# The last head's probabilities by transfers, the network's first half first, and TensorE's order written out to the end

## The chip, the core and the metric

The kernel runs on one core of a Trainium2 chip. A core has five engines that run side by side, each through its own queue of instructions in order: TensorE (matmuls and their weight loads; PE and PEld in the profile), VectorE (DVE), ScalarE (ACT), GpSimd (POOL) and SyncE (SP), which here issues the transfers (DMA). Engines wait for each other through semaphores. TensorE writes to PSUM, which VectorE and ScalarE read; everything else lies in SBUF. The metric is the device time of one execution in microseconds; before the change it is 1357.93 us, the median of 3 runs (1357.65 to 1358.64).

## The reference

One pre-norm transformer layer over 1024 tokens of 512 features, in float32, with 32 heads of 128:

```python
x = x + attention(layernorm(x), wq, wkv, wo)
x = x + ffn(layernorm(x), k0, s0, k1, s1, k2, s2)

# attention: q, k, v = products with wq, wkv
scores = einsum('bqhd,bkhd->bhqk', q[..., :DN], k) * scale
scores = where(causal, scores, NEG_INF)
attn = einsum('bhqk,bkhd->bqhd', softmax(scores), v).reshape(B, S, H * DV)
return einsum('bse,ed->bsd', attn, wo)

# ffn: conn_dense(k, x) = x @ where(k, 1, -1); ei_dense also weighs the last fifth of the inputs
h = relu(s0 * conn_dense(k0, x)) * 2
h = relu(ei_dense(h, k1, s1, P)) * 2
return ei_dense(h, k2, s2, P)
```

The second layer norm needs a token's whole row, that is, the output of all heads for that token; the network then works on each token alone.

## The kernel before

*Tiles.* The 1024 tokens are 8 tiles of 128 (`NT`), in two halves of 4 (`TPB`, half `qb` 0 and 1). Heads go in pairs (`G` = 2, 16 pairs). The main loop (line 689) has one step for each head and query tile: `steps` lists `(h, qt)`.

*One softmax step* (`probabilities`, line 503). TensorE writes the scores of query tile `qt` against the keys it may see, `(qt + 1) * 128` columns, to the PSUM tile `sc`. There is one such tile (pool `ps_sc`, one buffer), so the next step's scores wait until this one has been read. VectorE adds the mask and takes the row minimum of the negated scores (line 518, `nmax`); ScalarE takes the exponential and its row sum (529), VectorE the reciprocal (533), ScalarE scales (534).

*Turning the probabilities.* The product with v needs the keys on the partitions, so each tile has to be transposed. For heads 0 to 30 `transpose_blocks` (540) transposes blocks of 32 x 32 on VectorE into the tile `tb0` or `tb1` (for a half), and `exchange` (575), once a half is complete, moves the blocks to their places in `pT0` or `pT1` with 16 transfers on SP's queue. `attend` (588) follows 4 steps (half 0) or 6 steps (half 1) after that: its matmuls `ps_av` and a VectorE copy (619) give `attn`. For head 31 `transpose_last` (548) does whole transposes of 128 x 128 on TensorE (568) into PSUM, copied out by VectorE (573) and ScalarE (571); its query tiles run in the order 4 to 7, then 0 to 3 (line 632), and `attend` takes another branch (596 to 608).

*What fills TensorE between.* In each step the loop adds parts of two other chains: the products that make q, k and v of the next pair (`products`, seven a matrix, with sums on VectorE and ScalarE), and the output product of an earlier pair. For the last two pairs the latter is `o_unit(g, t)` (490): two matmuls for token tile `t`, added into `acc` (501), which also holds the residual. How many parts are due by a step is planned by `out_by`, `chain_end` and a count of columns (`done`, `goal`, `total`).

*The network* (from line 772). `transposed_input(k)` takes the layer norm of the four tiles of half `k`, transposes them on TensorE (`ptx_f`), and splits them in a high and a low part (`hi` on ScalarE, `lo` on VectorE); `hidden_layer` and `output_layer` multiply both parts with the sign weights, which GpSimd makes from `k0`, `k1`, `k2` in `sign_weights`. The order is: half 1 in, hidden layer 0 of half 1, half 0 in, hidden layer 1 of half 1, hidden layer 0 of half 0, output of half 1, hidden layer 1 of half 0, output of half 0.

*What sets the order.* Transfers stand in SP's queue in program order (`load`, 64). `keep_order` (68) pins an instruction to its place in the program while `pinned[0]` is true; matmuls and transposes on TensorE go through it. `pinned[0]` is set to false for the last 8 steps and what follows (line 692), where a scheduler in the build places instructions on all engines. VectorE, ScalarE and GpSimd are placed by that scheduler except in the first stage. Once built, each engine's order is fixed.

Of the kernel before, what the change touches and what calls it, by code (L numbers as in the profile page):

```python
# [8 lines left out]
F32 = mybir.dt.float32  # L9
F32R = mybir.dt.float32r  # L10
# [19 lines left out]
def kernel(  # L30
# [30 lines left out]

    pinned = [False]

    def load(dst, src):

        tc.keep_in_program_order(nc.sync.dma_start(dst, src))

    def keep_order(ins):
# [131 lines left out]
    def mean_var(mv, xt, name):  # L200

        if len(xt.shape) == 2:
            stats = small.tile([P, 6], F32, tag="stats", name=f"stats_{name}")
            keep_order(nc.vector.bn_stats(stats, xt))
        else:
            stats = small.tile([P, 2, 6], F32, tag="stats2", name=f"stats_{name}")
            for half in range(2):
                nc.vector.bn_stats(stats[:, half, :], xt[:, half, :])
        keep_order(nc.vector.bn_aggr(mv, stats))

# [11 lines left out]

    def normalise(xt, mean_rstd, name):
        xn = work.tile([P, D], F32, tag="p", name=f"xn_{name}")
        dst = xn if len(xt.shape) == 2 else xn.rearrange("p (h d) -> p h d", h=2)
        nc.vector.tensor_scalar(dst, xt, *mean_rstd, ALU.subtract, ALU.mult)
        return xn

# [13 lines left out]
    def input_statistics(t):  # L242
        mean_var(mv_a[:, t, :], x_in[:, t, :], f"a{t}")
        keep_order(
            nc.scalar.activation(std_a[:, t, :], mv_a[:, t, 1:2], AF.Sqrt, bias=eps)
        )

    def input_rows(t):
        keep_order(nc.vector.reciprocal(rstd_a[:, t, :], std_a[:, t, :]))
        keep_order(  # L250
            nc.vector.tensor_scalar(
                x_in[:, t, :],
                x_in[:, t, :],
                mv_a[:, t, 0:1],
                rstd_a[:, t, :],
                ALU.subtract,
                ALU.mult,
            )
        )

    def input_columns(t):
        pt = transposed(t, x_in[:, t, :], "a")
        keep_order(nc.scalar.copy(xnT[:, :, t * P : (t + 1) * P], pt))

# [46 lines left out]
    def qk_plain(between):  # L311
# [6 lines left out]
        for n_units in range(NT * 2 * G):  # L318
# [17 lines left out]
            if i == TPB - 1:  # L336
                keep_order(
                    nc.scalar.activation(
                        (qT, kT)[which][h][:, k * QB : (k + 1) * QB],
                        banks[n],  # L340
                        AF.Copy,
                        scale=(-scale, 1.0)[which],
                    )
                )
# [198 lines left out]

    last_pT = {}

    def transpose_last(qt, p):
        qb, i = divmod(qt, TPB)
        if i == 0:  # L550
            spare = (heads, "qT"), (heads, "qT"), (heads, "kT"), (heads, "v")
            bufs = {"kT": 3, "v": 3}
            if qb == 0:
                t = keep.tile([P, 2, 2, TPB, P], F32, tag="tb0", name="pT_last0")
                last_pT[qb] = [t[:, m] for m in range(2)]
            else:
                last_pT[qb] = [
                    pl.tile(
                        [P, 2, TPB, P], F32, tag=tag, name=f"pT_last{m}", bufs=bufs.get(tag)
                    )  # L560
                    for m, (pl, tag) in enumerate(spare)
                ]
        for m in range(qt // 2 + 1):
            chunks = range(2 * m, min(2 * m + 2, qt + 1))
            n = len(chunks)
            ps = ps_st.tile([P, 2, P], F32, tag="st", name=f"ps_pT{qt}_{m}")
            for kc in chunks:
                nc.tensor.transpose(ps[:, kc % 2, :], p[:, kc * P : (kc + 1) * P], ident)
            dst = last_pT[qb][m][:, :n, i, :]
            if m % 2:  # L570
                nc.scalar.copy(dst, ps[:, :n, :])
            else:
                nc.vector.tensor_copy(dst, ps[:, :n, :])

    def exchange(h, qb):
# [12 lines left out]
    def attend(h, qb, pT):  # L588
# [6 lines left out]
        dst = attn[h, qb]  # L595
        if h == H - 1:
            ps = ps_mm.tile([P, TPB, P], F32, tag="mm", name=f"ps_av{h}_{qb}")
            for kc in range(nk):
                first = max(0, kc - qb * TPB)
                matmul(  # L600
                    ps[:, first:, :],
                    lhsT=vs[h][:, kc, :],
                    rhs=last_pT[qb][kc // 2][:, kc % 2, first:, :],
                    start=(kc == 0),
                    stop=(kc == nk - 1),
                )
            nc.vector.tensor_copy(dst.rearrange("p (t i) -> p t i", t=TPB), ps)
            return
        ps = ps_mm.tile([P, NB, TPB, B32], F32, tag="mm", name=f"ps_av{h}_{qb}")
# [18 lines left out]

    steps = [(h, qt) for h in range(H) for qt in range(NT)]
    steps[-NT:] = [(H - 1, (qt + TPB) % NT) for qt in range(NT)]
    to_attend = {}
    w_sign = {}

    def softmax_step(h, qt):
        p = probabilities(h, qt)
        if h < H - 1:
            transpose_blocks(h, qt, p)
        else:  # L640
            transpose_last(qt, p)

# [7 lines left out]
    PRODUCT, O_PART = 2.0, 1.0  # L650
    ATTEND_AFTER = (TPB, TPB + 2)

    pinned[0] = True
    def first_blocks():
        for t in tb:
            keep_order(nc.vector.memset(t, 0.0))
        softmax_step(*steps[0])
# [13 lines left out]
        }  # L671
    )
    load_o_weights(0)

# [14 lines left out]
    for i, (h, qt) in enumerate(steps):  # L689
        g, j = divmod(h, G)  # L690
        s = i % (G * NT)
        pinned[0] = i + 1 < len(steps) - NT
        if s == 0:
            n_chain = 21 if g + 1 < NG else 7
            o_cols = O_PART if g + 1 < NG else 2 * O_PART
            n_out = 0 if g == 0 else 14 if g + 1 < NG else NT

            if g + 2 < NG:
                out_by = [max(0, (14 * (t - 2) + 12) // 13) for t in range(G * NT)]
            elif g + 2 == NG:  # L700
                out_by = [0, 0, 0, 2, 4, 6, 6, 8, 10, 12, 13, 14, 14, 14, 14, 14]
            else:
                out_by = [max(0, t - NT + 1) for t in range(G * NT)]
            done, chain_done, out_done = 0.0, 0, 0
            total = (
                2 * G * sum(score_cols(t) for t in range(NT))
                + PRODUCT * n_chain
                + o_cols * n_out
            )
            chain_end = 14 if g + 1 < NG else 6  # L710
        if s == 0:
# [61 lines left out]
        if h == H - 1:  # L773
            if qt == 0:
                attend(h, 1, None)
            if qt == 1:
                for t in range(TPB, NT):
                    o_unit(g, t)
        if h == H - 1 and s == NT:
# [23 lines left out]
    x_parts, h1, h2 = {}, {}, {}  # L803
    for k, tag in ((1, "pT1"), (0, "tb1")):
        x_k = keep.tile([P, 2, NC, QB], F32R, tag=tag, name=f"x{k}")
        x_parts[k] = h2[k] = (x_k[:, 0], x_k[:, 1])
    h1[1] = (part(keep, "pT0", "h1_hi1"), part(pairs, "wraw", "h1_lo1", 2))

    def transposed_input(k):
        tiles = range(k * TPB, (k + 1) * TPB)  # L810
        stats = statistics([xs[t] for t in tiles], f"f{k}")
        hi, lo = x_parts[k]
        for t, st in zip(tiles, stats):
            pt = transposed(t, normalise(xs[t], st, f"f{t}"), "f")
            cols = slice((t % TPB) * P, (t % TPB + 1) * P)
            nc.scalar.copy(hi[:, :, cols], pt)
            nc.vector.tensor_tensor(
                lo[:, :, cols], pt, hi[:, :, cols].bitcast(F32), ALU.subtract
            )

    n_ps = [0]
# [7 lines left out]
    def hidden_layer(i, k, src, dst):  # L829
        hi, lo = dst  # L830
        for oc in range(NC):
# [13 lines left out]
            nc.vector.tensor_copy(h_hi, h)  # L845
            nc.vector.tensor_tensor(h_lo, h, h_hi.bitcast(F32), ALU.subtract)

    def output_layer(k):
# [30 lines left out]
    h1[0] = (part(keep, "tb0", "h1_hi0"), part(heads, "qT", "h1_lo0", 2))  # L879
# [42 lines left out]
```

## Time and profile before

| | us |
|---|---|
| median of 3 runs | 1357.93 |
| the profiled execution, its time | 1358.12 |
| its span, first to last instruction | 1356.34 |
| TensorE busy | 1342.3 |
| VectorE busy | 807.6 |
| ScalarE busy | 496.5 |
| GpSimd busy | 262.5 |

The page gives each engine's busy time, and then groups of instructions: line, engine, operation, what is written and read, how many, busy time and the mean of one, and the engine's idle time before them with what ended it. A matmul in float32 is two passes in the trace. The chain of waits is followed back from the last instruction to what released each step. In a timeline a row has the start and the length in us from the span's start. Most of TensorE's groups have line 74, the helper that records every matmul, so they are told apart by the tile they write: `sc` scores, `ps_av` the product with v, `ps_o` output units, `ps_pT` the transposes of head 31, `ptx_f` those of the network's input, `ps_h` and `ps_out` its layers.

### The profile page before, as it was taken

To read this page: it belongs to the slowest core of one execution; us is meant where nothing else is said; L and a number is where in the kernel's file an instruction comes from. 1 tells how busy PE (TensorE), PEld (TensorE's weight loads), DVE (VectorE), ACT (ScalarE), POOL (GpSimd) and SP (SyncE) were. 2 spreads that over 40 slices of the span, in tenths; PEclk is the share of its full clock that TensorE was granted. 3 is DMA by queue.
4 is the path that set the end of the run, shared out by engine and by line. 5 is a ranking of instruction groups with operands and counts; after the bars stand their busy time and mean duration, and the time that the engine had idled before them with its cause. 6 is when DMAs were issued, how large, how long until landed. Compare 5 with 4: busy or idle time off the path is not lost.

```text
span 1356.3 us, 16289 instructions
## 1 busy us (share of the span) xinstructions
PE 1342.3 (99%) x5564; PEld 869.7 (64%) x5564; DVE 807.6 (60%) x1661; ACT 496.5 (37%) x922; POOL 262.5 (19%) x324
## 2 busy tenths in 40 slices
PE   8999999999999999999999999999999999999998
PEld 7747575665757566575756657575665756657567
DVE  5455565656656565565656566565656556686475
ACT  3434333333433333343433333333333333335321
POOL 3411122211212221021222102122120212110200
PEclk9999999999999999999999999999999999999999
DMA  5356454445646444564644556454455645446301
GB/s 187 78 109 125 89 127 96 95 97 103 140 84 129 97 88 101 109 141 80 129 93 88 108 109 127 87 127 94 88 116 109 127 83 118 87 83 128 67 0 63
DMA packets 259506, 139.26 MB, mean 103 GB/s; under 512 B 18272, under 2 KB 253280, under 8 KB 259424
## 3 DMA queue, kind: packets, MB, share of 16 engines
q1 hardware_dynamic: 259424, 138.22, 48.6%
q8 instruction: 45, 0.74, 0.2%
q14 instruction: 37, 0.30, 0.1%
HBM read 38.54 MB, written 2.10 MB: 30 GB/s over the span
## 4 chain that ended last, share of the span: by engine, by line
PE 99%; DVE 0%; DMA 0%; ACT 0%; issue 0%; ACTq 0%
PE sc L74 18%; PE ps_av L74 18%; PE ps_o L74 15%; PE Y_v L74 6%; PE Y_k L74 6%; PE Y_q L74 6%; PE Z_v L74 4%; PE X_v L74 4%; PE X_q L74 4%; PE Z_q L74 4%; PE Z_k L74 4%; PE X_k L74 4%; PE ps_qk L74 2%; PE ps_h L74 2%; PE ps_out L74 1%; PE ptx_a L232 0%
## 5 line engine op out<-in xcount | busy, mean ns | idle before, releaser
L529 ACT ACTIVATE p<-p,nmax 128x128 f32<-128x128 f32 (+7 forms) x256 | 198.4, 775 | 675.3 <-DVE nmax L518 673.2
L74 PE MATMUL sc<-kT,qT 128*128 128x512 f32 (+3 forms) x768 | 290.1, 487 | 1.4 <-DVE nmax L518 1.4
L74 PE MATMUL ps_av<-pT,v 128*128 128x512 f32 x744 | 250.3, 486 | 0.0
L518 DVE CUSTOM_DVE_ANT_0 p<-sc,mask 128x128 f32<-128x128 f32 (+7 forms) x256 | 191.3, 747 | 90.4 <-PE sc L74 90.4
L540 DVE STREAM_TRANSPOSE tb<-p 128x128 f32<-128x128 f32 (+1 forms) x248 | 187.3, 769 | 75.5 <-ACT p L534 72.0
L534 ACT ACTIVATE p<-p,rtotal 128x128 f32<-128x128 f32 (+7 forms) x256 | 196.5, 773 | 78.5 <-DVE rtotal L533 78.4
L74 PEld LDWEIGHTS ps_av<-pT,v 128*128 128x128 f32 x744 | 141.1, 190 | 127.7 <-issue 103.0
L74 PEld LDWEIGHTS sc<-kT,qT 128*128 128x128 f32 x768 | 138.7, 190 | 90.0 <-issue 77.5
L481 DVE TENSOR_TENSOR acc<-acc,ps_o 128x512 f32<-128x512 f32 x190 | 128.7, 683 | 56.1 <-PE ps_o L74 50.9
L74 PE MATMUL ps_o<-wo,attn 128*128 128x256 f32 (+1 forms) x400 | 110.7, 414 | 0.3 <-DVE attn L619 0.3
L533 DVE RECIPROCAL rtotal<-total 128x1 f32<-128x1 f32 x256 | 40.5, 158 | 112.8 <-ACT p L529 112.4
L74 PEld LDWEIGHTS ps_o<-wo,attn 128*128 128x128 f32 x400 | 73.3, 190 | 31.0 <-issue 24.2
L442 POOL TENSOR_TENSOR at<-attn,attn 128x512 f32<-128x512 f32 x14 | 17.7, 1267 | 348.4 <-DVE attn L619 348.4
L619 DVE COPY attn<-ps_av 128x512 f32<-128x512 f32 x62 | 42.2, 681 | 49.8 <-PE ps_av L74 49.8
L74 PEld LDWEIGHTS X_v<-wv,xnT 128*128 128x128 f32 x512 | 62.2, 192 | 5.1
L74 PE MATMUL X_v<-wv,xnT 128*128 128x128 f32 x512 | 62.3, 275 | 0.0
L74 PEld LDWEIGHTS ps_o<-osum,at 128*128 128x128 f32 x224 | 42.5, 190 | 22.8 <-issue 19.1
L74 PE MATMUL X_q<-xnT,wq 128*128 128x512 f32 x120 | 56.4, 593 | 0.0
L74 PE MATMUL X_k<-xnT,wk 128*128 128x512 f32 x120 | 56.4, 592 | 0.0
L291 POOL TENSOR_TENSOR wsumk<-wk 128x256 f32<-128x256 f32 x15 | 10.9, 727 | 234.3 <-PE Z_v L74 156.0
L74 PE MATMUL ps_o<-osum,at 128*128 128x256 f32 x224 | 55.0, 379 | 0.0
L529 ACT ACTIVATION_READ_ACCUMULATOR p<-p,nmax 128x1 f32 x256 | 47.7, 186 | 0.0
(146 smaller groups left out, 1637.3 us busy)
## 6 DMA issues: line engine op xcount, KB each, us to landing
pT<-tb SPq DMA_DIRECT2D x496, 128.0 KB, 3.1
pT<-tb SPq DMA_DIRECT2D x496, 64.0 KB, 2.1
wq<-in_L_attn_wq_dram SPq DMA_DIRECT2D x32, 256.0 KB, 3.3
wk<-in_L_attn_wkv_dram SPq DMA_DIRECT2D x32, 256.0 KB, 3.9
wv<-in_L_attn_wkv_dram SPq DMA_DIRECT2D x16, 512.0 KB, 4.0
wo<-in_L_attn_wo_dram SPq DMA_DIRECT2D x16, 512.0 KB, 3.7
x_in<-_attn_hidden_states_dram SPq DMA_DIRECT2D x8, 256.0 KB, 5.3
acc<-_attn_hidden_states_dram SPq DMA_DIRECT2D x8, 256.0 KB, 6.6
```

What stands on the lines that cost most here:

```text
L74: keep_order(nc.tensor.matmul(*args, **kw))
L291: nc.gpsimd.tensor_tensor(t[:, 0], a(1, 0), a(1, 1), ALU.add)
L442: nc.gpsimd.tensor_tensor(t0, b(0, 1), b(0, 0), ALU.subtract)
L481: nc.vector.tensor_tensor(dst, dst, ps, ALU.add)
L518: nc.vector.tensor_tensor_reduce(out=p[:, :n], in0=sc[:, :n], in1=mask[:, S - n :], scale=1.0, scalar=BIG, op0=ALU.add, op1=ALU.min, accum ...
L529: nc.scalar.activation(p[:, :n], p[:, :n], AF.Exp, bias=nmax, scale=-1.0, accum_out=total)
L533: nc.vector.reciprocal(rtotal, total)
L534: nc.scalar.activation(p[:, :n], p[:, :n], AF.Copy, scale=rtotal)
L540: nc.vector.transpose(tb[qb][:, : qt + 1, :, i, :], p[:, :n].rearrange("p (c b k) -> p c b k", b=NB, k=B32))
L619: nc.vector.tensor_copy(dst.rearrange("p (t a i) -> p a t i", a=NB, i=B32), ps)
```

## The change

Head 31 is treated as the other heads: `transpose_last` and its branch of `attend` go, its query tiles run from 0 to 7, and its probabilities go through `tb0`, `tb1` and two exchanges. Of the last pair `attend` for half 0 comes 6 steps after the half is complete, in place of 4. The plan of the last pair is another (`out_by`, `chain_end` 9 in place of 6): five of the eight output units of the pair before are handed out during the steps, three are left for the end. After the loop half 0 comes first: `attend` of head 31's half 0, the four output units of half 0 with the layer norm of each tile by itself (`network_input`, statistics of one tile in place of four), whose transposes and splitting (`columns`) stand among the output units; then hidden layer 0 of half 0, `attend` of half 1 and its four units, hidden layer 1 of half 0 with the four transposes of half 1 after its third group, hidden layer 0 of half 1, output of half 0, hidden layer 1 of half 1, output of half 1. `pinned[0]` stays true to the end, so all of TensorE's order is that of the program; the pins on VectorE and ScalarE in the first stage go through `keep_first`, which stops after that stage. Several of the network's tiles lie in other buffers.

```diff
+    def keep_first(ins):
+        if first_stage[0]:
+            tc.keep_in_program_order(ins)
...
-    def transpose_last(qt, p):
...
-            for kc in chunks:
-                nc.tensor.transpose(ps[:, kc % 2, :], p[:, kc * P : (kc + 1) * P], ident)
...
-    steps[-NT:] = [(H - 1, (qt + TPB) % NT) for qt in range(NT)]
...
     def softmax_step(h, qt):
-        p = probabilities(h, qt)
-        if h < H - 1:
-            transpose_blocks(h, qt, p)
-        else:
-            transpose_last(qt, p)
+        transpose_blocks(h, qt, probabilities(h, qt))
...
-    ATTEND_AFTER = (TPB, TPB + 2)
+    def attend_after(h, qb):
+        return TPB if qb == 0 and h < H - 2 else TPB + 2
...
-        pinned[0] = i + 1 < len(steps) - NT
...
-                out_by = [max(0, t - NT + 1) for t in range(G * NT)]
+                out_by = [0, 0, 1, 1, 2, 2, 3, 3, 4, 4, 4, 5, 5, 5, 5, 5]
...
-            chain_end = 14 if g + 1 < NG else 6
+            chain_end = 14 if g + 1 < NG else 9
...
-        if qt % TPB == TPB - 1 and h < H - 1:
+        if qt % TPB == TPB - 1:
             qb = qt // TPB
-            to_attend[i + ATTEND_AFTER[qb]] = (h, qb, exchange(h, qb))
+            to_attend[i + attend_after(h, qb)] = (h, qb, exchange(h, qb))
...
+    def network_input(t):
+        k, i = divmod(t, TPB)
+        pl, tag, bufs = (work, "p", 3) if k == 0 else (heads, "kT", 3) if i < 3 else (heads, "qT", 4)
+        xn = pl.tile([P, D], F32, tag=tag, name=f"xn_f{t}", bufs=bufs)
+        normalise(xn, xs[t], statistics([xs[t]], f"f{t}_")[0])
+        hi, lo = x_parts[k]
+        cols = slice(i * P, (i + 1) * P)
+        def columns():
+            pt = transposed(t, xn, "f")
+            nc.scalar.copy(hi[:, :, cols], pt)
+            nc.vector.tensor_tensor(
+                lo[:, :, cols], pt, hi[:, :, cols].bitcast(F32), ALU.subtract
+            )
+        return columns
...
-    attend(H - 1, 0, None)
-    transposed_input(1)
-    for t in range(TPB):
-        o_unit(NG - 1, t)
-    hidden_layer(0, 1, x_parts[1], h1[1])
-    transposed_input(0)
-    hidden_layer(1, 1, h1[1], h2[1])
...
-    hidden_layer(0, 0, x_parts[0], h1[0])
-    output_layer(1)
-    hidden_layer(1, 0, h1[0], h2[0])
-    output_layer(0)
+    first, second = (to_attend[i] for i in sorted(to_attend))
+    attend(*first)
+    columns = {}
+    for t in range(TPB):
+        o_unit(NG - 1, t)
+        columns[t] = network_input(t)
+        if t >= 2:
+            columns[t - 2]()
+    next(o_chain)
+    columns[2]()
+    next(o_chain)
+    columns[3]()
+    next(o_chain)
+    for _ in hidden_layer(0, 0, x_parts[0], h1[0]):
+        pass
+    attend(*second)
+    for t in range(TPB, NT):
+        o_unit(NG - 1, t)
+        columns[t] = network_input(t)
+    for oc, _ in enumerate(hidden_layer(1, 0, h1[0], h2[0])):
+        if oc + 2 == NC:
+            for t in range(TPB, NT):
+                columns[t]()
+    for _ in hidden_layer(0, 1, x_parts[1], h1[1]):
+        pass
+    output_layer(0)
+    for _ in hidden_layer(1, 1, h1[1], h2[1]):
+        pass
+    output_layer(1)
```

More of the change, by code (lines that the diff above doesn't have):

```diff
@@ L60 @@
     wo_v = wo.rearrange("(h p) d -> p h d", p=P)
-    pinned = [False]
+    pinned, first_stage = [False], [True]
     def load(dst, src):
         tc.keep_in_program_order(nc.sync.dma_start(dst, src))
+    def keep_first(ins):
+        if first_stage[0]:
+            tc.keep_in_program_order(ins)
     def keep_order(ins):
@@ L203, in mean_var @@
             stats = small.tile([P, 6], F32, tag="stats", name=f"stats_{name}")
-            keep_order(nc.vector.bn_stats(stats, xt))
+            keep_first(nc.vector.bn_stats(stats, xt))
         else:
@@ L208, in mean_var @@
                 nc.vector.bn_stats(stats[:, half, :], xt[:, half, :])
-        keep_order(nc.vector.bn_aggr(mv, stats))
+        keep_first(nc.vector.bn_aggr(mv, stats))
     def statistics(tiles, name):
@@ L221, in statistics, with normalise @@
         return [(mv[:, t, 0:1], rstd[:, t, :]) for t in range(n)]
[L223 to L227, printed above, removed]
+    def normalise(xn, xt, mean_rstd):
+        nc.vector.tensor_scalar(
+            xn.rearrange("p (h d) -> p h d", h=2), xt, *mean_rstd, ALU.subtract, ALU.mult
+        )
     def transposed(t, xn, name):
@@ L243, in input_statistics @@
         mean_var(mv_a[:, t, :], x_in[:, t, :], f"a{t}")
-        keep_order(
+        keep_first(
             nc.scalar.activation(std_a[:, t, :], mv_a[:, t, 1:2], AF.Sqrt, bias=eps)
@@ L248, in input_rows @@
     def input_rows(t):
-        keep_order(nc.vector.reciprocal(rstd_a[:, t, :], std_a[:, t, :]))
-        keep_order(
+        keep_first(nc.vector.reciprocal(rstd_a[:, t, :], std_a[:, t, :]))
+        keep_first(
             nc.vector.tensor_scalar(
@@ L262, in input_columns @@
         pt = transposed(t, x_in[:, t, :], "a")
-        keep_order(nc.scalar.copy(xnT[:, :, t * P : (t + 1) * P], pt))
+        keep_first(nc.scalar.copy(xnT[:, :, t * P : (t + 1) * P], pt))
     def B(j, k):
@@ L336, in qk_plain @@
             if i == TPB - 1:
-                keep_order(
+                keep_first(
                     nc.scalar.activation(
@@ L542, in transpose_blocks @@
         )
-    last_pT = {}
-    def transpose_last(qt, p):
[L549 to L555, printed above, removed]
-            else:
[L557 to L566, printed above, removed]
-            for kc in chunks:
[L568 to L573, printed above, removed]
     def exchange(h, qb):
@@ L595, in attend @@
         dst = attn[h, qb]
[L596 to L608, printed above, removed]
         ps = ps_mm.tile([P, NB, TPB, B32], F32, tag="mm", name=f"ps_av{h}_{qb}")
@@ L636, in softmax_step @@
     def softmax_step(h, qt):
-        p = probabilities(h, qt)
-        if h < H - 1:
-            transpose_blocks(h, qt, p)
-        else:
-            transpose_last(qt, p)
+        transpose_blocks(h, qt, probabilities(h, qt))
     def score_cols(qt):
@@ L655, in first_blocks @@
         for t in tb:
-            keep_order(nc.vector.memset(t, 0.0))
+            keep_first(nc.vector.memset(t, 0.0))
         softmax_step(*steps[0])
@@ L672 @@
     )
+    first_stage[0] = False
     load_o_weights(0)
@@ L772 @@
                 next(sum_chain, None)
[L773 to L778, printed above, removed]
         if h == H - 1 and s == NT:
@@ L803 @@
     x_parts, h1, h2 = {}, {}, {}
[L804 to L811, printed above, removed]
+    x_parts[0] = h2[0] = (part(keep, "tb0", "x0_hi"), part(keep, "pT0", "x0_lo"))
+    h1[0] = (part(pairs, "wraw", "h1_hi0", 2), part(heads, "qT", "h1_lo0", 2))
+    for parts, tag in ((x_parts, "tb1"), (h1, "pT1")):
+        both = keep.tile([P, 2, NC, QB], F32R, tag=tag, name=f"half1_{tag}")
+        parts[1] = (both[:, 0], both[:, 1])
+    h2[1] = x_parts[1]
+    def network_input(t):
[3 more added lines that the diff above has]
+        normalise(xn, xs[t], statistics([xs[t]], f"f{t}_")[0])
         hi, lo = x_parts[k]
-        for t, st in zip(tiles, stats):
-            pt = transposed(t, normalise(xs[t], st, f"f{t}"), "f")
-            cols = slice((t % TPB) * P, (t % TPB + 1) * P)
+        cols = slice(i * P, (i + 1) * P)
+        def columns():
+            pt = transposed(t, xn, "f")
             nc.scalar.copy(hi[:, :, cols], pt)
@@ L846, in hidden_layer @@
             nc.vector.tensor_tensor(h_lo, h, h_hi.bitcast(F32), ALU.subtract)
+            yield
     def output_layer(k):
@@ L870, in output_layer @@
             nc.sync.dma_start(out_v[:, t, :], osb)
-    attend(H - 1, 0, None)
-    transposed_input(1)
+    first, second = (to_attend[i] for i in sorted(to_attend))
+    attend(*first)
+    columns = {}
     for t in range(TPB):
         o_unit(NG - 1, t)
-    hidden_layer(0, 1, x_parts[1], h1[1])
-    transposed_input(0)
-    hidden_layer(1, 1, h1[1], h2[1])
-    h1[0] = (part(keep, "tb0", "h1_hi0"), part(heads, "qT", "h1_lo0", 2))
-    hidden_layer(0, 0, x_parts[0], h1[0])
+        columns[t] = network_input(t)
[21 more added lines that the diff above has]
+        pass
     output_layer(1)
-    hidden_layer(1, 0, h1[0], h2[0])
-    output_layer(0)
 _INS = [
```

## The prediction

> **What bounds the kernel now.** I read the page's busy times first, then what TensorE waited for, then the chain of waits in order of time, and then single rows in the last 140 us, where the two kernels differ. Times like 1281.3 are us from the span's start.
>
> ```profile
> PE 1342.3 (99%) x5564; PEld 869.7 (64%) x5564; DVE 807.6 (60%) x1661; ACT 496.5 (37%) x922; POOL 262.5 (19%) x324
> ...
> PEclk9999999999999999999999999999999999999999
> ```
>
> TensorE is busy for 99% of the span at full clock: only its work and its waits count. Its waits (us in total, times, longest):
>
> ```profile
> PE ptx_a L232 <- DVE x_in L251: 5.8, 1, 5.8
> PE ptx_f L232 <- DVE xn_f L226: 1.5, 1, 1.5
> PE sc L74 <- DVE nmax L518: 1.4, 1, 1.4
> ...
> PE ptx_f L232 <- DVE x L817: 0.5, 1, 0.5
> PE ps_o L74 <- DVE attn L619: 0.3, 1, 0.3
> ```
>
> The 5.8 (start), the 1.4 and a 0.7 lie in stages left alone. The change can win back 1.5, 0.5 and 0.3, and TensorE work. The chain (start, length, what) shows both:
>
> ```profile
> 1250.79 0.61 PE ps_pT L568 x5
> ...
> 1254.62 0.66 PE ps_pT L568 x6
> ...
> 1275.66 5.61 PE ps_av L74 x16
> 1281.27 0.02 issue
> 1281.30 0.70 DVE attn L619
> ...
> 1292.61 2.17 PE ps_av L74 x8
> 1294.78 0.02 issue
> 1294.80 0.69 DVE attn L607
> ...
> 1345.01 7.54 PE ps_out L74 x32
> ```
>
> Each `ps_pT` transpose takes 0.66/6 = 0.11 us of TensorE. A wait row counts from the modelled end of a matmul, some 0.16 after the next could have been issued, so I count lost issue time: 0.50 before 1282.04, 1.61 before 1296.22, 0.84 inside the `ptx_f` group, and 0.24 in the last layer (7.54 against 7.30 for the other `ps_out` group). Sum 3.19.
>
> **The change, part by part.** Up to TensorE's second score group of head 30 (1220.45) all orders are the same; after it:
>
> *Removed.* 36 transposes x 0.109 = 3.94 us of TensorE, on the bounding path; also 18 PSUM copies on VectorE and ScalarE, beside TensorE's work. The attention products, output units and network keep count and shape.
>
> *Added beside TensorE.* Eight STREAM_TRANSPOSEs on VectorE (0.31 to 1.25 us) and 32 transfers on SP's queue.
>
> *Fixed order.* Score tiles share one PSUM tile (`ps_sc`, one buffer), so a score group waits until VectorE has reduced the one before. Walking TensorE's new order with the old groups' lengths (a product of v 1.78, a full score tile 1.72, output unit 1.72, `ps_av` 2.16 or 5.59), the waits are:
>
> ```profile
> 1228.02 0.65 DVE L518 CUSTOM_DVE_ANT_0 p<-sc,mask 128x512 f32<-128x512 f32 x1
> 1228.60 0.08 DVE L518 DVE_READ_ACCUMULATOR2_ANT nmax<- 128x1 f32 x1
> ...
> 1248.43 1.25 DVE L540 STREAM_TRANSPOSE tb<-p 128x1024 f32<-128x1024 f32 x1 [0.22 <-ACT p L534]
> ...
> 1284.07 0.69 DVE L501 TENSOR_TENSOR acc<-acc,ps_o 128x512 f32<-128x512 f32 x1 [1.75 <-PE ps_o L74]
> 1284.79 0.75 DVE L208 BATCH_NORM_STATS2 stats_f<-acc 128x6 f32<-128x256 f32 x2
> 1285.57 0.21 DVE L209 BATCH_NORM_AGGREGATE mv_f<-stats_f 128x2 f32<-128x12 f32 x1
> ```
>
> These VectorE rows (start, length, line, operation) give the reduction of a 512-wide tile (0.65, + 0.08 for its minimum), a full tile's transpose, and the addition and statistics of one output tile (1.71 from the start of one to the next).
>
> 1. Head 30's tile 2 comes one product earlier and catches up with the reduction: 0.2.
> 2. Head 31's tiles 3 and 4 stand side by side. Tile 3 leaves TensorE at 1257.5; VectorE first copies `attn30_0` (0.69), then reduces (0.65 + 0.08): tile 4 starts at 1258.7. Lost 1.25 (0.9 if VectorE were free).
> 3. Tiles 5 and 6 likewise: drain 0.2, reduction 0.96 + 0.08. Lost 1.2.
> 4. `ps_av31_0` and the first output unit. TensorE: tile 4 1258.7, + 1.08 + unit 1.72 + tile 5 1.29 + wait 1.2 + tile 6 1.51 + `ps_av30_1` 5.59 + tile 7 1.72 = 1272.9. Transfers:
>
> ```profile
> 1199.82 9.61 SPq L66 DMA_DIRECT2D pT<-tb  x15
> ...
> 1249.74 11.07 SPq L66 DMA_DIRECT2D pT<-tb  x16
> 1261.21 1.74 SPq L66 DMA_DIRECT2D k<-in_L_ffn_k_dram  x3
> ```
>
> A 64 KB transfer is issued each 0.64 us and lands 2.1 after, a 128 KB one each 0.69 and lands 3.1 after (medians of the page's transfer rows). Head 30's second half starts at 1250.3 (0.6 later than before, as head 31's tile 0 cuts into its softmax); + 11.07 for its 16 issues + 1.74 for the three sign loads = 1263.1; + 15 x 0.644 + 2.1 = 1274.9. So `ps_av31_0` waits 2.0. But the unit behind it needs `attn31_0`, and its copy stands behind tile 7's STREAM_TRANSPOSE on VectorE. From a full score tile's end to its transpose's end the old head 30 took 1249.68 - 1244.31 = 5.4: 1272.9 + 5.4 = 1278.3, + copy 0.69 = 1278.95. From 1272.9 to there TensorE has 2.15 + 0.86 of work: lost 3.1 in all. Transfers may land 0.7 later at no cost; beyond that each us counts.
>
> The Trainium skill bears on this: DMA: Bandwidth & Descriptors, section Anatomy of one DMA, fits 2.0 us + bytes / 436 GB/s (for the GpSimd path), which for this 1 MB together would be an estimated 4.4, not 11.8. The row decides, since 16 issues in turn are what takes long. By the page `ps_av31_0` would not wait, and the unit would still wait until 1278.95: the same sum.
>
> 5. `ptx_f0`. VectorE adds unit 0, takes its statistics, then those of unit 1, then normalises: 2 x 1.71 + 0.17 + 0.69 + 0.54, so `xn_f0` is ready 4.65 after 1280.05, at 1284.7; TensorE has units 1 and 2 meanwhile, to 1283.25. Lost 1.45. A smaller one of the same kind follows: 0.3.
> 6. `ptx_f4` to `ptx_f7` stand side by side with three banks. The fourth waits for ScalarE's cast (0.59) and VectorE's subtraction (0.69, behind a cast and a subtraction of the hidden layer): 1.4. In the old order they were spread.
> 7. Last layer: the old order puts two products of the next tile before the last one of the first; in the fixed order it waits for cast and subtraction: 0.5, in place of 0.24. Two waits under 0.1: 0.1.
>
> Sum 0.2 + 1.25 + 1.2 + 3.1 + 1.45 + 0.3 + 1.4 + 0.5 + 0.1 = 9.5.
>
> *Costed at nothing.* The exchange of queries 512 to 1023: issued from 1278.3, landed by 1278.3 + 15 x 0.69 + 3.1 = 1292; `ps_av31_1` comes at 1301, after seven units, four `ptx_f` and hidden layer 0 (7.46). Slack 9; without that layer it would still be 1.5. The sign weights on POOL (7.36 us, from 1265 as before) are needed at 1293. The results' transfers of the first half go out earlier, and the last ends as before.
>
> Balance: 9.5 - 3.19 - 3.94 = **+2.4 us**. The profiled execution took 1358.12 for a span of 1356.34 (1.78 around it): 1358.7 + 1.8 = 1360.5. The median of the runs is 0.19 under that execution, so the forecast is **1360.3**. Laid out the same way, the old order's last 130 us come out within 0.3 of the trace, which is my error for fixed durations. Bounds of the waits: 7.9 if VectorE is free wherever it could be (2, 3, 6 at 0.9 each), so +0.8; above, the transfers.
>
> **The rivals.** What a measurement of this kernel can tell from no change is about 0.2%, 2.7 us, so the forecast itself is "no change", at its slow edge.
>
> *Late transfers (slower).* Place: `ps_av31_0`. It is the mechanism beyond 1275.7:
>
> ```profile
> L66 SPq DMA_DIRECT2D pT<-tb x992: 585/602/2068, 52.5 to 1260.1; - x199
> ...
> DMA to landing us min/median/max: 2.0/2.7/5.2
> ```
>
> One issue in some exchanges takes up to 2.07 instead of 0.60, and two exchanges are in series here. Before, no TensorE wait came of it (0.2 in all). One long issue of 1.5 eats the slack and costs 0.75: +3.2. Two cost 2.25: +4.6, 1362.5. It decides from one issue longer by 1.1.
>
> *A colder clock (slower).* From 1272.9 to 1284.7 TensorE loses 4.6 of 11.8 us. The row speaks against harm: waits of 1.5 and 0.8 at 1295 left the granted clock at 1.00 in the window 1282 to 1306. But the Trainium skill, TensorE: Matmul & The Clock Gate, Part 1, says that about 3.4 us of idle window halves the clock until a busy window has passed, and advises against gaps over 3. The longest unbroken gap here is 2.0, so by row and by rule the sum stays; were the stretch counted as idle all the same, 3.4 us at half clock lose 1.7: 1362.
>
> *Nothing takes the old waits' place (faster).* Then -3.94 - 3.19: 1350.8. For it: heads 0 to 30 run by the same exchange with no wait. Against it: there, products and output parts stand between the score groups; here they are used up.
>
> *Milder waits (no change).* VectorE free at 2, 3 and 6, or part of 5 hidden: +0.8, or with 5 halved 0: 1358 to 1359.
>
> **How the numbers follow.** The forecast as worked out: 0.70. It lies 0.3 below the bound; with transfers a little late (half of the exchanges have a long issue) 0.25 of the 0.70 falls beyond. Late by over one long issue 0.08, clock 0.04, milder 0.14, faster 0.04. Slower by over 0.2%: 0.25 + 0.08 + 0.04 = 0.37. Within: 0.45 + 0.14 = 0.59. Faster: 0.04. The range 1358.8 to 1362.0 leaves out the faster case, the lower half of the milder one, and two long issues; the forecast's own is 1359.5 to 1361.3.
>
> **What would show it.** No `ps_pT`; TensorE's waits listing `sc <- nmax` anew with 1.0 to 1.2 each, twice (the listed gaps are 0.16 shorter than mine); a wait of `ps_av` on a transfer near 1273, 1.5 to 2; `ps_o <- attn` near 1278, about 0.8; `ptx_f <- xn_f` 1.3 near 1283; `ptx_f` on VectorE 1.2 near 1321. Wrong if `ps_av31_0` starts after 1275.7, if the clock column shows under 9 in the last slices, or if VectorE serves tiles 3 and 5 late.

## The result, and the profile after

The changed kernel takes **1361.20 us** (median of 9 runs, 1359.97 to 1362.94), against 1357.87 before (9 runs, 1357.48 to 1358.64): a ratio of 1.0025, with a 95% interval of 1.0016 to 1.0034. It is 3.3 us slower. The forecast was 1360.3 with a range of 1358.8 to 1362.0, so the time lies in the range, but just beyond the 0.2% bound (1360.65), on the side that had 0.37 and not on the likeliest one, "within". The single times say more than the median: before they keep within 1.2 us, after they spread over 3 and leave a hole, 1359.97 to 1361.20 (five) and 1362.36 to 1362.94 (four). The middle of the lower five is 1360.33; with one run more in the upper group the median would have lain above the range.

The profiled execution took 1360.83 for a span of 1359.1 (before 1358.12 and 1356.34), so it belongs to the lower group. Its busy times and its clock row, from the page:

```profile
PE 1339.8 (99%) x5528; PEld 865.7 (64%) x5528; DVE 808.6 (59%) x1663; ACT 495.7 (36%) x920; POOL 262.7 (19%) x324
...
PEclk9999999999999999999999999999999999999999
```

36 matmuls fewer and 2.5 us less busy TensorE in a span that is 2.7 longer: TensorE waits more. What it waited for after 1220 us (us in total, times, longest):

```profile
PE ps_av L79 <- DMA pT<-tb: 2.7, 1, 2.7
PE sc L79 <- DVE nmax L522: 2.1, 2, 1.1
PE ptx_f L236 <- DVE xn_f L229: 1.2, 1, 1.2
PE ptx_f L236 <- DVE half_tb L773: 1.1, 1, 1.1
PE ps_out L79 <- DVE half_tb L804: 0.2, 1, 0.2
```

These are the waits that the prediction listed: the transfers ahead of `ps_av31_0`, two score tiles, `ptx_f0`, `ptx_f7`, the last layer. Only `ps_o <- attn` is missing. The chain of waits (start, length, what) shows why:

```profile
1273.70 2.06 DMA pT<-tb
1275.76 0.38 issue
1276.13 2.40 PE ps_av L79 x8
1278.53 1.92 PE ps_o L79 x4
...
1285.11 0.66 PE ptx_f L236 x4
...
1322.53 0.66 PE ptx_f L236 x4
...
1349.26 6.02 PE ps_out L79 x25
```

The sixteenth transfer of head 31's first half landed at 1275.76, where 1274.9 was predicted. By the time `ps_av31_0` and its copy were through, tile 7's transpose no longer stood in the way. SP's queue, in the timeline:

```profile
1250.46 11.30 SPq L66 DMA_DIRECT2D pT<-tb  x16
1262.17 1.70 SPq L66 DMA_DIRECT2D k<-in_L_ffn_k_dram  x3
1263.98 25.70 SPq L66 DMA_DIRECT2D pT<-tb  x32
```

The start was 0.16 later than worked out, the sixteen issues took 0.23 longer, and from their end to the next exchange 2.22 passed in place of 1.74: together 0.87, the lateness of the landing. Of the last 0.48, 0.40 is the pause between the sixteenth issue and the first sign load. The rows of the kernel before have the same pause (1249.74 + 11.07 is 1260.81, the next row starts at 1261.21); the prediction left it out of its sum. From the landing to the first matmul another 0.37 went by.

Counted as in the prediction (from 0.16 before a matmul's modelled end to the start of the next, gaps of 0.08 and more), TensorE lost this much after 1215 us:

| step of the prediction | predicted | trace after |
|---|---|---|
| 1. tile 2 of head 30 | 0.2 | 0.11 |
| 2. tiles 3 and 4 of head 31 | 1.25 | 1.19 |
| 3. tiles 5 and 6 | 1.2 | 1.22 |
| 4. `ps_av31_0` and first unit | 2.0 + 1.1 | 2.90 + 0.09 |
| 5. `ptx_f0`, and a smaller one | 1.45 + 0.3 | 1.40 + 0.19 |
| 6. `ptx_f4` to `ptx_f7` | 1.4 | 0.13 + 1.30 |
| 7. last layer, small waits | 0.5 + 0.1 | 0.48 + 0.09 |
| new waits | 9.5 | 9.1 |
| old waits, in the trace of before | 3.19 | 2.91 |

With 3.94 for the transposes the traces give 9.1 - 2.9 - 3.9 = +2.3; the spans differ by 2.7. Of the remaining 0.4, 0.23 was there before the orders part (score tile 0 of head 30 starts at 1218.30, before at 1218.07), and the rest lies in gaps under 0.08 and in the error of counting.

So the profiled execution is accounted for. Not accounted for by it are the times above 1362: both profiles of this kernel belong to lower times. The experiments take them up.

### The profile page after: what moved, and what is told of

It is laid out like the page before. It is cut to its first block, busy times and chain, and to the rows that moved or that the text cites. A ratio compares the mean times of both kernels' runs of the same rounds, so it can differ in the third digit from the quotient of the medians.

```text
span 1359.1 us, 16258 instructions
## 1 busy us (share of the span) xinstructions
PE 1339.8 (99%) x5528; PEld 865.7 (64%) x5528; DVE 808.6 (59%) x1663; ACT 495.7 (36%) x920; POOL 262.7 (19%) x324
## 4 chain that ended last, share of the span: by engine, by line
PE 97%; DVE 1%; SPq 1%; DMA 0%; ACT 0%; issue 0%; DVEq 0%; ACTq 0%
PE sc L79 18%; PE ps_av L79 18%; PE ps_o L79 14%; PE Y_v L79 6%; PE Y_k L79 6%; PE Y_q L79 6%; PE Z_v L79 4%; PE X_v L79 4%; PE X_q L79 4%; PE Z_q L79 4%; PE Z_k L79 4%; PE X_k L79 4%; PE ps_qk L79 2%; PE ps_h L79 2%; PE ps_out L79 1%; SPq L66 1%
## 5 line engine op out<-in xcount | busy, mean ns | idle before, releaser
L79 PE MATMUL ps_av<-pT,v 128*128 128x512 f32 (+3 forms) x768 | 258.4, 486 | 2.8 <-DMA pT<-tb 2.7
L544 DVE STREAM_TRANSPOSE tb<-p 128x128 f32<-128x128 f32 (+7 forms) x256 | 193.1, 769 | 77.7 <-ACT p L538 74.0
L79 PEld LDWEIGHTS ps_av<-pT,v 128*128 128x128 f32 x768 | 145.7, 190 | 135.4 <-issue 109.7
```

What stands on the lines that cost most here:

```text
L79: keep_order(nc.tensor.matmul(*args, **kw))
L544: nc.vector.transpose(tb[qb][:, : qt + 1, :, i, :], p[:, :n].rearrange("p (c b k) -> p c b k", b=NB, k=B32))
```

## The experiments

All are edits of the changed kernel, timed in alternation with the kernel before (median of the latter 1358.1 to 1358.3 in these sets). "Lost" is counted as in the table.

**The changed kernel again** (run again). No edit.

> The changed kernel once more, to see its spread beside the kernels that follow. Theory (transfers): ps_av31_0 starts when the sixteenth transfer of head 31's first half has landed, with no slack left, so every late transfer shows in the time: median 1361.2 as before, single times over some 3 us (1360 to 1363), while the kernel before keeps within 1.2. Rival (clock): the times above 1362 go with a lower granted clock; then they stay in every kernel of this set alike.

Measured: median 1362.22 (8 runs: 1360.30, 1360.41, 1360.79, 1361.63, 1362.81, 1362.99, 1363.67, 1363.76), ratio 1.0031 (1.0020 to 1.0042). There are low and high times again, and this median lies above the predicted range. The profiled run, 1360.79, lost 9.16 and shows a clock of 1.00 until its work ends. The times alone settle nothing between the theories. The mean granted clock of each run says more: it is 0.998 for 1361.63 and 0.997 for 1363.67 and 1363.76, and no lower than 0.999 for the others. What that shows is read over all runs at the end of this section.

**Does the transfer or the copy decide at `ps_av31_0`?** (run signs_later)

```diff
-        if h == H - 1 and s == NT:
+        if h == H - 1 and s == NT + TPB - 1:
             big = [
...
```

> The three sign-weight loads are issued after the first-half exchange of head 31, not ahead of it, so the exchange starts and ends 1.7 us earlier (landed 1274.0 in place of 1275.76). Step 4 of the prediction says that the copy of attn31_0, queued on VectorE behind the transpose of tile 7 (to 1279.3), then decides: ps_av31_0 waits 1.1 in place of 2.7, and the lost time comes back as a wait ps_o <- attn of about 2.5; the span is 1358.9 to 1359.1 (0 to -0.2), and the single times draw together to about 1 us with a median near 1360.5. Rival (transfers alone decide): -1.7, span 1357.4, median 1359.5. Rival (clock): spread stays 3 us.

Measured: median 1360.61 (16 runs, 1359.95 to 1361.20), ratio 1.0019 (1.0011 to 1.0026). TensorE's waits after 1220 us:

```profile
PE ps_o L79 <- DVE attn L579: 2.1, 1, 2.1
PE sc L79 <- DVE nmax L522: 2.1, 2, 1.1
...
PE ps_av L79 <- issue: 0.5, 1, 0.5
```

The transfers landed at 1272.99, and the wait moved to the copy of `attn31_0` behind tile 7's transpose, as step 4 said: lost 0.65 + 2.26 = 2.91 in place of 2.99. Taking 2.1 us off the landing (counted from the start of tile 4) won next to nothing of the undisturbed time: its span of 1358.2 is 0.8 shorter, but 0.7 of that was there at tile 4. "Transfers alone decide" falls. But the group above 1362 is gone, and the spread is that of the kernel before. The single gap of 2.9 had become two, of 0.65 and 2.26.

**Is there slack left?** (run three_more)

```diff
+            if (h, qb) == (H - 1, 0):
+                extra = small.tile([P, 3], F32, tag="extra", name="extra", bufs=1)
+                for c in range(3):
+                    load(extra[:, c : c + 1], s0[None, :].to_broadcast((P, 1)))
             to_attend[i + attend_after(h, qb)] = (h, qb, exchange(h, qb))
```

> Three more small transfers are issued ahead of the first-half exchange of head 31, 1.8 us of SP's queue. Prediction's step 4: 0.7 of lateness is free, so +1.1 (span 1360.2, median 1362.3). Theory from the trace of the changed kernel: the landing at 1275.76 and 0.37 from there to the first matmul had used the slack up, so +1.7 to +1.8 (span 1360.8, median 1363.0). Rival (hidden transfer): 0.

Measured: median 1364.45 (5 runs, 1363.04 to 1365.18), ratio 1.0046 (1.0034 to 1.0059): more than either theory. The landing was 1.6 later, counted from the start of tile 4, and `ps_av31_0` 1.3 later. The rest stands in the clock. Windows of three_more (us, busy PE, PEld, DVE, ACT and POOL, granted clock, DMA share, GB/s), and the chain's row:

```profile
1274.00:1277.00 3.00, 0.14 (x1) 0.14 (x2) 0.48 (x4) 2.59 (x4) 0.00 (x0) 1.00 0.46 87
1277.00:1280.00 3.00, 3.00 (x6) 1.70 (x7) 1.05 (x1) 1.08 (x1) 0.00 (x0) 0.62 0.20 34
1280.00:1283.00 3.00, 3.00 (x9) 1.56 (x8) 0.96 (x2) 0.00 (x0) 0.00 (x0) 0.81 0.96 179
```

```profile
1276.86 3.82 PE ps_av L79 x8
```

After a gap of 4.2 the granted clock is at half, and the eight matmuls take 3.82 in place of 2.40. In windows of 0.2 us it is 0.50 from 1277.7 to 1281.1, 3.4 us, which at half speed is 1.7 us of work lost.

**Is it the gap that does that?** (runs filled and three_more_2) The kernel of three_more, and TensorE given something to do in the gap:

```diff
+    spare = ps_mm.tile([P, NC, P], F32, tag="mm", name="ps_spare")
+    for c in range(24):
+        keep_order(nc.tensor.transpose(spare[:, c % NC, :], ident, ident))
     attend(*first)
```

> As three_more (three more transfers ahead of head 31's first-half exchange), with 24 transposes of the identity matrix (2.6 us of TensorE, output unused) put between tile 7 of head 31 and ps_av31_0. They need nothing and end at 1275.5, ahead of the landing near 1276.9, so they delay nothing; TensorE's gap falls from 4.0 to 1.3. Theory (a gap of some 3 to 4 us halves the clock for the 3.4 us that follow): ps_av31_0 takes 2.4 again in place of 3.82, span 1359.6, median 1362.6 to 1362.9 (three_more: 1361.3 and 1364.45). Rival (only the lateness of the transfers costs): no change.

> three_more once more, beside filled: median 1364.5 with all single times above 1363, clock 0.998 in the mean.

Measured: filled 1362.01 (8 runs, 1361.63 to 1363.00), three_more once more 1363.31 (5 runs, 1361.79 to 1365.16). The same windows of filled, and its chain:

```profile
1274.00:1277.00 3.00, 1.59 (x15) 1.35 (x13) 0.48 (x4) 2.48 (x4) 0.00 (x0) 1.00 0.51 97
1277.00:1280.00 3.00, 2.79 (x10) 1.66 (x10) 1.50 (x2) 1.20 (x1) 0.00 (x0) 1.00 0.16 28
1280.00:1283.00 3.00, 3.00 (x8) 1.25 (x7) 1.75 (x4) 0.00 (x0) 0.00 (x0) 1.00 0.97 178
```

```profile
1275.09 2.07 DMA pT<-tb
1277.21 2.42 PE ps_av L79 x8
```

TensorE has *more* to do, starts `ps_av31_0` 0.2 later than three_more (counted from tile 4), and ends 1.2 earlier: the clock stays at 1.00 and the matmuls take 2.42. So the gap costs twice, as a wait and through the clock after it. The profile of the repeated three_more shows the fall at its largest, 6.8 us at half from 1276.0 to 1282.8, `ps_av31_0` 4.64. Its lowest time, 1361.79, breaks the expectation that all lie above 1363: that run's mean clock is 1.000, so even after a gap of about 4 the fall does not come every time.

**The changed kernel's own gap, shortened.** (run unit_in_gap)

```diff
+    next(o_chain)
     attend(*first)
     ...
-    next(o_chain)
     for _ in hidden_layer(0, 0, x_parts[0], h1[0]):
```

> One output unit of the pair before (1.72 of TensorE) is moved from behind ptx_f2 to between tile 7 of head 31 and ps_av31_0; the transfers are as in the changed kernel. Theory (late transfers, and a clock that falls to half when the gap of TensorE gets past some 3 to 4 us, as in the run three_more): the gap falls from 2.8 to 1.1, so no time above 1362 remains: single times within 1359.5 to 1361.3, median 1360.3; the undisturbed profile gains only 0.4, since 0.5 of cover is lost behind ptx_f3. Rival (late transfers alone make the times above 1362): the same 3 us of spread, 0.4 lower.

Measured: median 1360.25 (21 runs, 1359.63 to 1361.18), ratio 1.0015 (1.0009 to 1.0022).

```profile
PE ps_av L79 <- DMA pT<-tb: 0.9, 1, 0.9
PE ps_h L79 <- issue: 0.7, 1, 0.7
```

The wait for the transfers is still there and as exposed to a late one as before, but none of 21 times is above 1361.2. So the times above 1362 come with the long gap; late transfers alone do not make them. The unit's cover was taken from elsewhere, where a wait of `ps_h` came: lost 8.56 in place of 9.1.

**Steps 2 and 3.** (run scores_apart) Sign loads as in signs_later, and other places for the units:

```diff
-                out_by = [0, 0, 1, 1, 2, 2, 3, 3, 4, 4, 4, 5, 5, 5, 5, 5]
+                out_by = [0, 0, 1, 1, 2, 2, 2, 2, 3, 3, 4, 5, 6, 6, 6, 6]
     ...
-    next(o_chain)
     for _ in hidden_layer(0, 0, x_parts[0], h1[0]):
```

> The sign loads after the exchange, as in the run signs_later, and output units of the pair before placed between the score tiles 3/4, 4/5 and 5/6 of head 31. Steps 2 and 3: both waits sc <- nmax of head 31 (1.1 + 1.0 listed) go. TensorE is then 0.7 earlier at the end of tile 7, and one unit fewer stands between the ptx_f groups, which costs 0.5 ahead of the first hidden layer: against signs_later (span 1358.2, median 1360.6) -1.1, so span 1357.1, median 1359.5. Rival: the additions of the units now stand ahead of the reductions on VectorE and the waits stay: 0.

Measured: median 1359.81 (21 runs, 1358.66 to 1360.18), ratio 1.0010 (1.0004 to 1.0017): 0.8 under signs_later. The waits:

```profile
PE ps_av L79 <- DMA pT<-tb: 1.5, 1, 1.5
PE ptx_f L236 <- DVE xn_f L229: 1.2, 1, 1.2
PE ptx_f L236 <- DVE half_tb L773: 1.1, 1, 1.1
PE ps_o L79 <- DVE attn L579: 1.0, 1, 1.0
PE ps_h L79 <- issue: 0.7, 1, 0.7
```

No `sc <- nmax` is left. Of its 2.4, half comes back at `ps_h`, for the unit that is now missing there; lost 7.86 against 9.02, so -1.16 where -1.1 was expected. (The span, 1358.4, is 1.3 longer than expected. This execution was that much later than the one of signs_later before the edit took hold: score tile 0 of head 30 starts at 1218.93, there at 1217.61.)

**Step 6.** (run ptx_spread)

```diff
-        if oc + 2 == NC:
-            for t in range(TPB, NT):
-                columns[t]()
+        if oc < 2:
+            columns[TPB + 2 * oc]()
+            columns[TPB + 2 * oc + 1]()
```

> ptx_f4, ptx_f5 stand after the first group of hidden layer 1 of half 0, ptx_f6, ptx_f7 after the second, in place of all four after the third. Step 6: the wait of ptx_f on VectorE (1.1 at 1321) goes, at most 0.2 comes in its place: span -1.0 to -1.3 (1357.9), median 1360.1. Rival: VectorE's subtractions are wanted by the hidden layer anyway and the wait moves to ps_h: 0.

Measured: lost 7.91 against 9.16 in the same set, so -1.25: 1.30 ahead of `ptx_f7` is gone, and 0.23 is left inside the group. Median 1359.42 (21 runs, 1358.69 to 1362.95), ratio 1.0015 (1.0008 to 1.0021). The spread stayed, as did the gap ahead of `ps_av31_0`.

**The fixed order undone.** (run scheduled)

```diff
         s = i % (G * NT)
+        pinned[0] = i + 1 < len(steps) - NT
```

> The order of TensorE from head 31 on is left to the scheduler, as in the kernel before; everything else as changed. Theory by the waits: three adjacent score tiles wait 1.0 to 1.3 in place of two, and the exchange of head 31's first half starts 1.7 later; the wait of ptx_f7 (1.1) and that of ps_out4 (0.4) are filled with other groups' products: span -0.7, median 1360.5 to 1361.5, with single times above 1362 still there since the gap ahead of ps_av31_0 stays at 2.4 to 2.9. Rival (the fixed order is what costs): 1357.

Measured: median 1361.74 (9 runs, 1360.93 to 1362.11), ratio 1.0026 (1.0016 to 1.0035).

```profile
PE sc L79 <- DVE nmax L522: 3.2, 3, 1.2
PE ps_av L79 <- DMA pT<-tb: 2.8, 1, 2.8
PE ptx_f L236 <- DVE xn_f L229: 1.2, 1, 1.2
```

Three score waits in place of two, and the waits of `ptx_f7` and `ps_out4` filled: lost 8.97 against 9.1, where 0.7 less was expected. The profile fell to half clock here (3.4 us from 1278.2) after a gap of 3.0. Two single times, 1362.01 and 1362.11, lie above 1362, as expected with the gap left in place. The fixed order is neither the gain nor the loss of this change; both orders lack the same cover.

**What the removed transposes were worth.** (run thirty_six) 36 transposes of the identity ahead of `attend(*second)`, written as in filled.

> 36 transposes of the identity (as many as the change removed) stand ahead of ps_av31_1, where TensorE waits for nothing. Removed-step of the prediction: 36 x 0.109 = 3.94 more: span 1363.0 against 1359.0, median 1365.2 to 1366.2. Rival (a part of them would be covered, and the removal won less): less than 3.5.

Measured: from the chain of waits,

```profile
1295.96 7.47 PE ps_h L79 x32
1303.43 3.93 PE ps_spare L850 x36
```

3.93 for 36, all on the path: the removal step stands (3.94). The median, 1364.24 (5 runs, 1363.75 to 1366.47), is 1 under what was expected, which had started from a median with falls of the clock in it. Four of the five have a mean clock of 1.000; their middle, 1364.04, is 3.7 above that of the changed kernel's lower five. The fifth is the profiled one, which fell, after a gap of only 2.74:

```profile
1276.28 3.97 PE ps_av L79 x8
```

**All waits covered.** (runs covered and covered_2) Units between the score tiles 3 to 7, `ps_av30_1` after tile 7, the sign loads after both exchanges, the second half's product and units ahead of the hidden layers, the transposes and the output groups spread (core of the edit):

```diff
-                out_by = [0, 0, 1, 1, 2, 2, 3, 3, 4, 4, 4, 5, 5, 5, 5, 5]
+                out_by = [0, 0, 1, 1, 2, 2, 2, 2, 3, 3, 4, 5, 6, 7, 7, 7]
...
     for t in range(TPB):
         o_unit(NG - 1, t)
         columns[t] = network_input(t)
+        if t == 2:
+            next(o_chain)
+            columns[0]()
+    columns[1]()
+    columns[2]()
+    attend(*second)
+    for t in range(TPB, NT):
+        o_unit(NG - 1, t)
+        columns[t] = network_input(t)
+        if t == TPB:
+            columns[3]()
+    for _ in hidden_layer(0, 0, x_parts[0], h1[0]):
+        pass
     for oc, _ in enumerate(hidden_layer(1, 0, h1[0], h2[0])):
+        for t in ((4, 5), (6,), (7,), ())[oc]:
+            columns[t]()
```

> All steps of the account answered at once: units between the score tiles 3 to 7 of head 31, ps_av30_1 after tile 7, sign loads after both exchanges, one unit ahead of ptx_f0, the second half's attention product between ptx_f2 and ptx_f3 and its units ahead of the first hidden layer, ptx_f4 to ptx_f7 spread, ps_out3 after the last hidden layer. By the account (steps 2 to 7 sum to 9.0, of which 2.5 to 3 come back as a wait for the second exchange near 1286): span 1353.7 to 1354.5, median 1355.5 to 1356.3, 5 under the changed kernel and 2 under the kernel before, single times within 1.3. Rival (waits move, none is won): 1359 to 1360.

Measured: median 1357.89 (13 runs, 1355.14 to 1359.05), ratio 0.9994 (0.9985 to 1.0002), 2 over what was expected. The lost time did fall as worked out, to 4.38, but 3.1 of it is one gap, ahead of `ps_av31_1`. The second exchange's last transfer landed at 1288.88, 0.30 before the matmuls start; the list of waits names an instruction of VectorE that had been done earlier. Then

```profile
1289.18 7.53 PE ps_av L79 x16
```

which takes 5.59 at full clock. The last edit keeps the waits and splits the gap, with one unit moved (`-` and `+` are against covered):

```diff
         if t == 2:
-            next(o_chain)
             columns[0]()
     columns[1]()
+    next(o_chain)
     columns[2]()
```

> As covered, but the last unit of the pair before stands between ptx_f1 and ptx_f2 in place of ahead of ptx_f0: the same waits in sum, in gaps of 1.3 to 2 in place of one of 3.3 to 3.9. Theory (clock after a long gap): ps_av31_1 takes 5.59 in place of 7.53; no times above 1357.2, median 1355.5 to 1356.0 (covered: 1357.89, 1355.14 to 1359.05). Rival (its late second exchange alone spreads covered's times): median and spread as covered.

Measured: median **1355.82** (21 runs, 1355.20 to 1356.77), ratio 0.9982 (0.9976 to 0.9989).

```profile
PE ps_av L79 <- DVE x_lo L773: 2.0, 1, 2.0
PE ptx_f L236 <- DVE xn_f L229: 1.2, 1, 1.2
PE ps_h L79 <- DVE h_lo L804: 0.2, 1, 0.2
```

```profile
1290.22 5.83 PE ps_av L79 x16
```

It lost 4.61, more than covered, and is 2.1 us faster in the median: gaps of 1.4 and 2.2 in place of one of 3.1. (Ahead of `ps_av31_1` the transfers landed at 1289.91 and VectorE's subtraction ended at 1290.08, so here the two limits are nearly level.) It beats the changed kernel by 5.4 us and the kernel before by 2.5.

**The clock of the single runs.** For every run the mean granted clock over its span is on record, to three digits. One stretch of 3.4 us at half clock takes 0.00126 off. The idle end of the program counts too: in the profiled run of the changed kernel the clock is at half from 1357.25 to the end of the span, 1.8 us, which makes 0.999 of a run without a fall. So 0.999 may be either. For 0.998 some 4.1 us at half are needed, and the span ends only 3.8 after the last matmul, so it needs a fall during the work; 0.997 needs two stretches.

| kernel | runs with 1.000 or 0.999 | runs with 0.998 or 0.997 |
|---|---|---|
| changed kernel, first set | all 9, 1359.97 to 1362.94 | none |
| the same again | 1360.30 to 1360.79 (3), 1362.81, 1362.99 | 1361.63, 1363.67, 1363.76 |
| ptx_spread | 1358.69 to 1360.64 (14) | 1360.99 to 1362.95 (7) |
| covered | 1355.14 to 1356.84 (6) | 1357.89 to 1359.05 (7) |
| three_more, both sets | 1361.79, 1363.06 | 1363.04 to 1365.18 (8) |
| scheduled | 1360.93 to 1361.97 (6) | 1361.74, 1362.01, 1362.11 |
| filled, signs_later, unit_in_gap, scores_apart, covered_2 | all 87 | none |
| kernel before, beside them | all 120, at 1.000 | none |

In ptx_spread and covered every run with 0.998 or 0.997 is slower than every other, and those with 0.997 are the slowest. The kernels whose gap was split or filled have no such run. In the changed kernel's first set the upper four have 0.999, and of the lower five four have 1.000; that fits one fall each, but does not prove it.

## Why the prediction was right, and where it was not

The forecast, 1360.3, is the time of the undisturbed runs (middle 1360.33), and the account of waits behind it is right. That the median of all runs stayed within the range is in part luck: in up to half of them the clock fell, a case to which the prediction had given 0.04, and the median of the second set, 1362.22, lies above the range.

*Removed* (3.94): right, 3.93 in thirty_six, where 36 transposes lie on the path with nothing to hide them.

*Steps 1 to 3*: right, 2.52 against 2.65. With units between the tiles the waits of steps 2 and 3 go, so the one score buffer behind VectorE's reduction is the cause. That the cover then lacks elsewhere is what "here they are used up" meant in the rival of no new waits.

*Step 4*: the sum was right (3.1 against 2.99), its split was not. The predicted 2.0 for the transfers was 2.9, since the last landing came 0.86 later than worked out, nearly half of it the pause of 0.40 that the sum left out, and the matmuls began 0.37 after landing, which it had at nothing; the predicted 1.1 for the copy was 0.09. That the two errors left the sum alone is luck: the two limits ended almost together. Both halves are limits in parallel, as signs_later shows. The free lateness of 0.7 was already spent.

*Steps 5 to 7*: right, 1.59, 1.43 and 0.57 against 1.75, 1.4 and 0.6. Step 6 is confirmed by ptx_spread. For step 5 covered and covered_2 are the test: they differ in one unit, and the wait of 1.40 ahead of `ptx_f0` is gone where the unit stands before it and back where it does not. Step 7 is read from the trace; in covered, where an output group stands behind the hidden layer, its wait is gone.

*Slips in the sums.* The terms printed for step 5 add up to 4.82, not 4.65; the trace has 4.6 from the first addition (1280.47) to `xn_f0`. Steps 2, 3 and 6 at 0.9 each give waits of 8.35, so +1.2, not 7.9 and +0.8. The old waits, counted in the one way used for the table, were 2.91 and not 3.19. None of this moves the forecast by more than 0.3.

*What was costed at nothing* held: no wait on the second half's exchange (landed at 1292.17, used at 1301.5), none on the sign weights.

*Where it failed* is the rival "a colder clock", which had 0.04. Its sentence was: "The longest unbroken gap here is 2.0, so by row and by rule the sum stays". The gap was 2.9, because of step 4's split, and the row that it rested on, waits of 1.5 and 0.8, was too short to test a longer one. Nor is the length of a gap what decides: after 2.74 the clock fell in thirty_six, after 2.90 and 2.96 it did not in the two profiles of the changed kernel.

The clock records of the traces show what does. The clock changes only on a grid of 3.413 us: stretches at half during the work last 3.413 us, or 6.827 in one run, and the stretches at full clock after a fall 61.44, 78.51 and 85.33, which is 18, 23 and 25 times as long. The grid is not tied to the program, for the first change of the clock comes between 10.5 and 13.6 us after the start of the span in the 14 profiles. The Trainium skill, TensorE: Matmul & The Clock Gate, Part 1, says the same: the window is 3413 ns and free-running. With the grid known from each trace, the idle time of TensorE can be read window by window. First again, then thirty_six, each with the two windows that hold the gap or follow it (us, busy PE, PEld, DVE, ACT and POOL, granted clock, DMA share, GB/s):

```profile
1271.30:1274.71 3.41, 1.97 (x7) 0.66 (x5) 1.99 (x4) 0.13 (x1) 2.08 (x4) 1.00 0.54 103
1274.71:1278.13 3.42, 2.07 (x7) 1.30 (x8) 1.07 (x2) 3.17 (x4) 0.00 (x0) 1.00 0.10 19
```

```profile
1272.63:1276.05 3.42, 1.07 (x3) 0.19 (x1) 1.31 (x3) 1.05 (x1) 0.92 (x2) 1.00 0.49 93
1276.05:1279.46 3.41, 3.18 (x5) 1.57 (x6) 1.41 (x2) 2.62 (x4) 0.00 (x0) 0.50 0.00 0
```

In again the gap is split between two windows, 1.44 and 1.35 idle; in thirty_six 2.35 of it lie in one, and the next window is at half clock. All profiles with a gap of over 2 us in the part where the kernels differ:

| run | gap | idle in its window(s) | clock after each |
|---|---|---|---|
| covered_2 | 2.19 | 0.75, 1.28 | 1.00, 1.00 |
| signs_later | 2.26 | 1.72 | 1.00 |
| ptx_spread | 2.91 | 1.25, 1.49 | 1.00, 1.00 |
| again | 2.96 | 1.44, 1.35 | 1.00, 1.00 |
| changed kernel | 2.90 | 1.94, 0.80 | 1.00, 1.00 |
| covered | 3.09 | 0.92, 2.12 | 1.00, 0.50 |
| thirty_six | 2.74 | 2.35 | 0.50 |
| scheduled | 3.00 | 2.45 | 0.50 |
| three_more | 4.17 | 1.46, 2.55 | 1.00, 0.50 |
| three_more_2 | 4.11 | 2.30, 1.65 | 0.50, 0.50 |

Up to 1.94 us idle in a window the next one is at full clock, from 2.12 on at half (1.65 was enough where the clock was at half already; at the idle end of the program, in unit_in_gap, 1.98 was). So the same gap counts in one run and not in the next, by where the grid cuts it. The bounds of the Trainium skill, no gaps over some 3.4 us (Part 1) and over 3 us (its section Why this matters for your kernels, which is where the prediction's "over 3" stands), are not safe ones by these runs.

The price in the rival, 1.7, was about right: from `ps_av31_0` to `ptx_f0` passed 8.98 in the changed kernel, and 1.5 to 1.6 more in three_more, thirty_six and scheduled. Without a fall the time is the lower group, with the forecast inside it; with one in up to half of the runs the median is the forecast plus 0.9.

*The rival of late transfers* looked right by its time (1362.5) but not by its cause: unit_in_gap leaves the transfers as late as they are and loses the upper group.

What stays open is where near 2 us the bound lies, and whether idle time in a window is the whole of it: no experiment set the idle time of a window by itself. The gaps of 2.19 and 2.26 could by their length put more than 2.12 into one window, but in 37 runs of covered_2 and signs_later no mean clock is under 0.999.

## What to carry to other kernels

Take the lost times from the trace row by row, as lengths in a new order: here seven terms came within 0.2 each. Read the pauses between the rows too: one of 0.40 was missed. Of two limits in parallel only the later one counts, so moving one wins no more than its distance to the other. Where TensorE must wait, prefer several short gaps to one long one, or put work that depends on nothing into it: covered_2 waits longer than covered and is 2.1 us faster. A spread of times in two groups is a hint to read the granted clock, of each run and behind the longest gap, before late transfers are blamed.

## What was not expected of the hardware

- A gap of TensorE of 2.7 to 3.1 us may or may not halve its granted clock: 1.00 after 2.90, 2.96 and 2.91 (the changed kernel twice, ptx_spread), 0.50 after 2.74, 3.00 and 3.09 (thirty_six, scheduled, covered). What separates them is the idle time within one window of a grid of 3.413 us, at most 1.94 against at least 2.12. The half clock set in between 1.7 us before work began again and 1.3 us after, and lasted one window, in one run with a gap of 4 us two.
- Between the landing of the last transfer and the first matmul that waited for it there were 0.3 to 0.4 us in most runs (0.37 after, 0.34 again, 0.35 in thirty_six), but 0.04 in three_more and filled. The cause was not looked for.
- The sixteen issues of an exchange took 11.30 in this kernel and 11.07 in the one before, with no single long issue among them: a queue's length has an error of its own, of some 2% here.
